# A transformer layer with experts on one core: the first chunk norms, their powers and the weight preparation reordered

## The chip, the cores and the metric

The kernel runs on one core of a Trainium2 chip. The metric is device time in microseconds (us), the median of several runs. A core has five engines that run side by side, each taking its own instructions in program order: PE (TensorE: matmuls and transposes into PSUM; PEld is its weight load), DVE (VectorE), ACT (ScalarE), POOL (GpSimd) and SP (SyncE, which here only issues DMA transfers). They wait for each other by semaphores.

## The reference

The input x is 32 sequences of 256 tokens with 128 features. It is normalised, and two branches read the result; the output is the sum of x and both. All is in float32.

```python
xn = layernorm(x)                                  # (x - m) / sqrt(v + 1e-5)
# branch A: 16 heads of 8; scores = cov(q, k)/8 + var(q) var(k)/8, softmax, Wo
# branch B:
hn   = layernorm(xn, ln1_w, ln1_b)
qkv  = hn @ in_proj_w.T + in_proj_b                # 16 heads of 8
attn = softmax(causal(q k / sqrt(8))) @ v          # over axis 0 of x: the 32 sequences are its positions
x1   = xn + attn @ out_proj_w.T + out_proj_b
hn2  = layernorm(x1, ln2_w, ln2_b)
# router: top 2 of 8 experts, gelu(hn2 @ w1[e]) @ w2[e], weighted by the gates
out  = x + A(xn) + x1 + experts(hn2)
```

The attention of branch B runs over the first axis of x, so its sequences are 32 long and there are 256 of them.

Two normalisations follow each other. With variance v of a token, the first scale is (v + eps)^-1/2. The variance of the normalised token is v/(v + eps), so the second scale is (v/(v + eps) + eps)^-1/2: both need only v.

## The kernel before, in words

The tokens are cut into 16 chunks of 512, each held as a tile of 128 partitions with four groups of 128 features (`[P, 4, P]`). `first_rounds` carries the chunks through branch B up to the router's logits in a software pipeline: its loop runs i from -2 to 15, and in one pass several chunks are at different stages. After it the heads of branch A are computed in a long loop (from about 270 us to the end), with routing, experts and combining woven in. Every engine executes its instructions in the order in which this code issues them (`manual_schedule`), so the order of the calls is the schedule.

Before the loop, in this order: `loads()` issues the DMA transfers of three chunks and the weights on the SP and ACT queues; `measure(0)` computes chunk 0's statistics; POOL casts two constants (`identb`, `causalb`); `norms(0)`; `set_in()`; `measure(1)`; `set_values(0)`.

The functions that matter:

- `measure(i)` (with `stats`): for each of the four groups a `bn_stats` and a `bn_aggr` on DVE (L262, L263; tiles sta and mva), then on POOL: add eps (L265), power -1/2 (L266), nb = -mean times scale (L274, L275), and the second scale r2 by two products, an add and a second power (L277 to L280). Eight POOL instructions of 128x4 elements each. `stats` serves the later normalisation of x1 too (stc, mvc, rsc).
- `norms(i)`: four ACT activations (L291) write the normalised tokens into zx; POOL multiplies them by r2 (L295) into zn.
- `turn_in(i)`: PE transposes the tokens (pta) and zn (ptb); ACT copies the first into xnT (L305) and scales the second into hT (L310); POOL adds the output bias `bout` to the tokens in place (L311).
- `project_in(i)`: PE computes pk, pq and pv from hT; ACT writes kb (L320), qT and v; an SP DMA writes v to DRAM, and `spread` brings it back into vb.
- `set_in()`: bk4 on DVE, four transposes of in_proj_w and out_proj_w on PE, copies to inT and outT on DVE. It then folds the value bias into the output bias: a broadcast copy bvs on DVE (L196), a product pbo on PE (L198), and an add to bout (L199).
- `set_rest()`: transposes and products of the weights of branch A on PE, with copies on DVE.
- `set_values(n)`: POOL fills v's column of ones (L244) and clears vb (L245); there are two buffers, n = 0 and 1. `set_second(n)`, in passes 3 to 5, fills the tiles of branch A on POOL (L225 to L232).
- `scores`, `lessened` (DVE: mx L374, pr L375), `exponents` (ACT), `turn_weights` (ptp, pT), `weigh` (po), `divide` (DVE: aden L412, o L413), `turn_out` (pto, oT), `project_out` (px on PE, x on DVE L426, then `stats` of x and a POOL add L429), `normalise` (POOL L436), `turn_normed`, `logits`.

A pass i issues, among other things: `load(i+5)`, `clear(i)` (an SP DMA that clears part of a DRAM buffer from the tile zero), `turn_in(i+2)`, `spread(i+1)`, `project_in(i+2)`, `project_out(i-1)`, in pass -2 `set_rest`, `set_values(1)` and the filling of zero, then `norms(i+3)`, `measure(i+4)`, `normalise(i-1)`, `scores(i+1)` and `lessened(i+1)`. So in a pass DVE has: x and the statistics of x1, then the statistics of chunk i+4, then the maxima of the next scores.

Of the kernel before, what the change touches and what calls it, by code (L numbers as in the profile page):

```python
# [11 lines left out]
F32 = mybir.dt.float32  # L12
BF16 = mybir.dt.bfloat16
I32 = mybir.dt.int32
AF = mybir.ActivationFunctionType
ALU = mybir.AluOpType
# [3 lines left out]
P = 128  # L20
NB = 32
SEQ = 256
NH, HD = 16, 8
NE, FF = 8, 256
NCHUNK = 16
# [3 lines left out]
EPS = 1e-5  # L29
# [39 lines left out]
def block_kernel(  # L69
# [21 lines left out]
    nc = tc.nc  # L91
# [6 lines left out]
    cp = ctx.enter_context(tc.tile_pool(name="cp", bufs=1))  # L98
# [26 lines left out]
    identb = cp.tile([P, P], BF16, name="identb")  # L125
    causalb = cp.tile([P, 32], BF16, name="causalb")
    bk4 = cp.tile([P, 4], F32, name="bk4")
    mhalf = cp.tile([P, 4, 1], F32, name="mhalf")
    wqkv = cp.tile([P, 3, P], F32, name="wqkv")
    wo = cp.tile([P, P], F32, name="wo")  # L130
    inT = cp.tile([P, 3, P], F32, name="inT")
# [49 lines left out]
    def set_in():  # L181
        nc.vector.tensor_scalar(bk4, cst[:, C_M4:C_M4 + 4], bk, None, ALU.mult)
        pt = bank_u([P, 4, P], "pt0")
        for n in range(3):
            nc.tensor.transpose(pt[:, n, :], ipw[:, n, :], ident)
        nc.tensor.transpose(pt[:, 3, :], opw, ident)
        nc.vector.tensor_copy(inT[:, 0:2, :], pt[:, 0:2, :])

        nc.vector.tensor_copy(
            inT[:, 2, :].rearrange("p (j g d) -> p j g d", j=4, g=4),  # L190
            pt[:, 2, :].rearrange("p (g j d) -> p j g d", j=4, g=4),
        )
        nc.vector.tensor_copy(outT, pt[:, 3, :])


        nc.vector.tensor_copy(bvs, bv.to_broadcast([P, P]))  # L196
        pbo = bank_u([P, P], "pbo")
        nc.tensor.matmul(pbo, bvs, outT, start=True, stop=True)  # L198
        nc.vector.tensor_tensor(bout, bout, pbo, ALU.add)  # L199

    def set_rest():
        pt = bank_w([P, 4, P], "pt1")
        nc.tensor.transpose(pt[:, 0, :], qkw[:, 0, :], ident)
        nc.tensor.transpose(pt[:, 1, :], qkw[:, 1, :], ident)
        nc.tensor.transpose(pt[:, 2, 0:NE], rw, ident[0:NE, 0:NE])
        nc.vector.tensor_copy(qkT, pt[:, 0:2, :])
        nc.vector.tensor_copy(rT, pt[:, 2, 0:NE])
        pb = bank_w([P, 2, P], "pqkw")
        for n in range(2):
            nc.tensor.matmul(pb[:, n, :], qkT[:, n, :], ccen, start=True, stop=True)  # L210
        nc.vector.tensor_copy(wqkv[:, 0:2, :], pb)


    NV, NQ = 3, 2
# [6 lines left out]
    def set_second(n):  # L221

        if n < NV:
            va = vaugs[n]
            nc.gpsimd.memset(va, 0.0)  # L225
            for h in range(2):
                nc.gpsimd.memset(va.rearrange("p i (m h) d -> p (i m) h d", h=2)[:, :, h, 16 + h:17 + h], 1.0)
        if n < 2:
            nc.gpsimd.memset(mts[n], 0.0)
            nc.gpsimd.memset(qkts[n], 0.0)  # L230
            for ti in range(2):
                nc.gpsimd.memset(qkts[n][:, ti, 1].rearrange("p g m r -> p (g m) r")[:, :, 9:10], 1.0)  # L232
# [7 lines left out]
    vs = [a1.tile([P, 4, 4, 4, HD + 1], F32, tag=f"v{n}", name=f"v{n}") for n in range(2)]  # L240
    vbs = [a1.tile([P, 4, 4, 16 * (HD + 1)], F32, tag=f"vb{n}", name=f"vb{n}") for n in range(2)]

    def set_values(n):
        nc.gpsimd.memset(vs[n].rearrange("p j k g d -> p (j k g) d")[:, :, HD:HD + 1], 1.0)  # L244
        nc.gpsimd.memset(vbs[n], 0.0)  # L245

    NZ = 32
# [9 lines left out]
    def stats(src, tag, i, bufs=2):  # L257

        st = a2.tile([P, 4, 6], F32, tag="st", name=f"st{tag}{i}")
        mv = a2.tile([P, 4, 2], F32, tag=f"mv{tag}", name=f"mv{tag}{i}")  # L260
        for k in range(4):
            nc.vector.bn_stats(st[:, k, :], src[:, k, :])  # L262
            nc.vector.bn_aggr(mv[:, k, :], st[:, k, :])  # L263
        rs = a2.tile([P, 4, 1], F32, tag=f"rs{tag}", name=f"rs{tag}{i}")
        nc.gpsimd.tensor_scalar(rs, mv[:, :, 1:2], EPS, None, ALU.add)  # L265
        nc.gpsimd.tensor_tensor(rs, rs, mhalf, ALU.pow)  # L266
        return mv, rs

    def measure(i):


        mv, rs = stats(xts[i], "a", i)
        nb = a2.tile([P, 4, 1], F32, tag="nb", name=f"nb{i}")
        nc.gpsimd.tensor_tensor(nb, mv[:, :, 0:1], rs, ALU.mult)  # L274
        nc.gpsimd.tensor_scalar(nb, nb, -1.0, None, ALU.mult)  # L275
        r2 = a2.tile([P, 4, 1], F32, tag="r2", name=f"r2{i}")
        nc.gpsimd.tensor_tensor(r2, rs, rs, ALU.mult)  # L277
        nc.gpsimd.tensor_tensor(r2, r2, mv[:, :, 1:2], ALU.mult)
        nc.gpsimd.tensor_scalar(r2, r2, EPS, None, ALU.add)
        nc.gpsimd.tensor_tensor(r2, r2, mhalf, ALU.pow)  # L280
        nrm[i] = rs, nb, r2

    def tokens(i):


        return zx[:, 4 * i:4 * i + 4]

    def norms(i):
        rs, nb, r2 = nrm.pop(i)
        for k in range(4):  # L290
            nc.scalar.activation(  # L291
                tokens(i)[:, k, :], xts[i][:, k, :], AF.Identity, bias=nb[:, k, :], scale=rs[:, k, :]
            )
        zns[i] = a2.tile([P, 4, P], F32, tag="zn", name=f"zn{i}")
        nc.gpsimd.tensor_tensor(zns[i], tokens(i), r2.to_broadcast([P, 4, P]), ALU.mult)  # L295

    def transposed(src, tag, i):
        pt = bank_u([P, 4, P], f"pt{tag}{i}")
        for k in range(4):
            nc.tensor.transpose(pt[:, k, :], src[:, k, :], ident)  # L300
        return pt.rearrange("p k t -> p (k t)")

    def turn_in(i):

        nc.scalar.copy(  # L305
            xnT[:, i, :].rearrange("p (c k s) -> p k c s", c=4, k=4),
            transposed(tokens(i), "a", i).rearrange("p (k c s) -> p k c s", k=4, c=4),
        )
        hTs[i] = a2.tile([P, 512], F32, tag="hT", name=f"hT{i}")
        nc.scalar.activation(hTs[i], transposed(zns.pop(i), "b", i), AF.Identity, bias=l1b, scale=l1w)  # L310
        nc.gpsimd.tensor_tensor(tokens(i), tokens(i), bout.unsqueeze(1).to_broadcast([P, 4, P]), ALU.add)  # L311

    def project_in(i):
# [137 lines left out]
    def chunk(i):  # L451
        return 0 <= i < NCHUNK

    def first_rounds():
        loads()
        nc.vector.memset(mhalf, -0.5)
        measure(0)
        nc.gpsimd.tensor_copy(identb, ident)
        nc.gpsimd.tensor_copy(causalb, cst[:, C_CAUSAL:C_CAUSAL + 32])
        norms(0)  # L460
        set_in()
        measure(1)
        set_values(0)
        for i in range(-2, NCHUNK):
            if chunk(i + 5):
                xts[i + 5] = load(i + 5)
            if 0 <= i < (NZ + 2) // 3:
                clear(i)
            if chunk(i + 2):
                turn_in(i + 2)  # L470
            if chunk(i - 1):
                weigh(i - 1, 1)
            if chunk(i):
                lessened(i, 2)
            if chunk(i - 1):
                divide(i - 1, 1)
            if chunk(i):
                lessened(i, 3)
                turn_weights(i, 0)
                turn_weights(i, 1)  # L480
                exponents(i, 1)
            if chunk(i - 1):
                turn_out(i - 1)
            if chunk(i + 1):
                spread(i + 1)
            if chunk(i + 2):
                project_in(i + 2)
            if i == NCHUNK - 1:
                project(0, 0)
                project_rest(0, 0)  # L490
            if chunk(i - 1):
                project_out(i - 1)
            if chunk(i):
                turn_weights(i, 2)
                turn_weights(i, 3)
            if i == -2:
                set_rest()
                set_values(1)
                nc.gpsimd.memset(zero, 0.0)
            if 3 <= i < 3 + NV:  # L500
                set_second(i - 3)
            if chunk(i + 3):
                norms(i + 3)
            if chunk(i + 4):
                measure(i + 4)
            if i == NCHUNK - 1:
                project(0, 1)
                project_rest(0, 1)
            if chunk(i - 1):
                normalise(i - 1)  # L510
            if chunk(i + 1):
                scores(i + 1)
            if chunk(i - 2):
                turn_normed(i - 2)
            if chunk(i + 1):
                lessened(i + 1, 0)
                lessened(i + 1, 1)
                exponents(i + 1, 0)
            if chunk(i):
                weigh(i, 0)  # L520
            if i == NCHUNK - 1:
                turn_qk(0)
            if chunk(i):
                divide(i, 0)
            if chunk(i - 2):
                logits(i - 2)
# [494 lines left out]
```

## Time and profile before

| what | value |
|---|---|
| median of three runs | 988.92 us (987.41 to 994.37) |
| the profiled execution | 992.8 us; first to last instruction (span) 991.0 us |
| mean granted TensorE clock | 0.976 of full speed |
| busy share of the span | PE 95%, DVE 71%, ACT 66%, POOL 57% |
| chain that ended last, by engine | PE 86%, DVE 7%, issue 2%, POOL 2%, ACT 1% |
| PE busy from 8 to 12, 24 to 28 and 36 to 40 us | 1.09, 1.12 and 1.52 of 4.00 us |
| POOL busy from 16 to 20, 20 to 24 and 24 to 28 us | 3.58, 4.00 and 3.75 of 4.00 us |
| POOL L295 (zn), mean of 16 | 1039 ns |
| POOL powers L266 (rsa) and L280, mean of 16 each | 1037 ns |
| ACT norms of a chunk (L291), four instructions | 1.65 us |

The busy shares are averages over stages with different limits; the change touches the first stage alone, so it is read from its rows. A line of a timeline gives the start, the duration, the engine, the line of the kernel, the operation, the tiles (written<-read), the shape and the count of merged instructions; in brackets stands how long the engine sat idle before it and what ended that. A line of the chain of waits gives start, duration and engine with tile. "issue" is time in which nothing that the profile shows was waited for.

### The profile page before, as it was taken

Reading aid. Unit: us, or ns where it says so; the run is one execution under the profiler, and the core shown is the slowest. Engines: PE = TensorE matmul, PEld = TensorE weight load, DVE = VectorE, ACT = ScalarE, POOL = GpSimd, SP = SyncE. Lnnn points to the kernel's source line nnn. Section 1 sums busy time; section 2 is a strip of 40 time slices with the busy share of each in tenths; the row PEclk is TensorE's granted clock in tenths of the full one; section 3 lists DMA queues with packets and bytes.
Section 4 is the critical chain, followed back from the end, with each engine's and each line's share of the span. In section 5 each row is a group of like instructions: output and inputs, shape, how many; then the busy total and the mean of one; then the engine's idle time right before and its main releaser. Section 6 shows DMA issues by size and latency. Waiting matters only on the chain.

```text
span 991.0 us, 32300 instructions
## 1 busy us (share of the span) xinstructions
PE 940.2 (95%) x13107; PEld 679.0 (69%) x13107; DVE 706.3 (71%) x1638; ACT 655.1 (66%) x1362; POOL 561.9 (57%) x725
## 2 busy tenths in 40 slices
PE   4788999989789999999999999999999999999998
PEld 2567777777666666666666689999866666666664
DVE  2477578667589999888888834444588888888882
ACT  4687878877446666666666665555666666676664
POOL 5468787785310002777777123333387888888870
PEclk9798999999889999999999999999999999999999
DMA  3344434422031000541111134444222321121220
GB/s 100 108 132 125 134 120 139 140 60 68 21 102 35 2 2 15 59 111 55 55 53 54 52 117 135 133 134 136 76 60 63 81 69 36 39 68 52 55 60 22
DMA packets 87747, 76.32 MB, mean 77 GB/s; under 512 B 32840, under 2 KB 70864, under 8 KB 87600
## 3 DMA queue, kind: packets, MB, share of 16 engines
q1 hardware_dynamic: 74736, 48.03, 17.4%
q0 software_dynamic: 11600, 26.10, 8.5%
q8 instruction: 103, 1.69, 0.7%
q10 hardware_dynamic: 1264, 0.14, 0.1%
q14 instruction: 44, 0.36, 0.1%
HBM read 33.98 MB, written 40.24 MB: 75 GB/s over the span
## 4 chain that ended last, share of the span: by engine, by line
PE 86%; DVE 7%; issue 2%; POOL 2%; ACT 1%; DMA 0%; ACTq 0%; DVEq 0%; SPq 0%; POOLq 0%
PE sm L610 26%; PE pav L634 13%; PE pe L854 6%; PE pp L557 6%; PE ph L845 6%; PE pqk L584 3%; PE ptp L300 2%; PE sT L616 2%; PE pt L653 2%; PE sc L359 2%; DVE pr L375 2%; PE px L834 2%; PE pk L316 2%; PE px L424 2%; PE py L687 2%
## 5 line engine op out<-in xcount | busy, mean ns | idle before, releaser
L625 ACT ACTIVATE ex<-sT 128x512 f32<-128x512 f32 x512 | 277.7, 595 | 179.0 <-PE sT L616 179.0
L622 DVE TENSOR_REDUCE mt<-sm 128x2 f32<-128x512 f32 x512 | 329.0, 686 | 73.6 <-PE sT L616 67.7
L610 PE MATMUL sm<-ka,qa 32*128 32x256 f32 x2048 | 292.4, 402 | 3.5 <-DVE mt L622 3.5
L616 PE MATMUL sT<-qa,ka 32*128 32x256 f32 x2048 | 291.0, 400 | 0.0
L610 PEld LDWEIGHTS sm<-ka,qa 32*128 32x128 f32 x2048 | 177.4, 185 | 81.0 <-issue 38.1
L616 PEld LDWEIGHTS sT<-qa,ka 32*128 32x128 f32 x2048 | 176.4, 184 | 2.6 <-issue 1.7
L801 POOL DMA_INDIRECT xsd<-zx,posi x128 | 122.9, 960 | 81.4 <-DVE posi L789 42.7
L905 POOL DMA_INDIRECT yg<-ysd,posb x128 | 122.1, 954 | 43.0 <-issue 31.5
L634 PE MATMUL pav<-ex,va 128*32 128x256 f32 x2048 | 137.2, 385 | 0.0
L859 POOL DMA_DIRECT2D ysd<-ye x71 | 48.2, 679 | 115.0 <-DVE ye L858 89.1
L634 PEld LDWEIGHTS pav<-ex,va 128*32 128x32 f32 x2048 | 53.8, 109 | 64.2 <-issue 24.0
L854 PEld LDWEIGHTS pe<-w,ge 128*128 128x128 f32 x568 | 74.5, 192 | 4.2 <-ACT ge L847 0.7
L854 PE MATMUL pe<-w,ge 128*128 128x128 f32 x568 | 74.9, 275 | 0.3 <-ACT ge L847 0.3
L845 PE MATMUL ph<-xT,w 128*128 128x256 f32 x284 | 73.3, 381 | 0.0
L557 PE MATMUL pp<-wqkv,xnT 128*128 128x384 f32 x128 | 65.6, 595 | 0.8 <-DVE mt L622 0.8
L858 DVE COPY ye<-pe 128x256 f32<-128x256 f32 x71 | 30.1, 424 | 50.8 <-PE pe L854 50.8
L837 ACT ACTIVATE xT<-px,vec 128x256 f32<-128x256 f32 x71 | 39.9, 563 | 35.8 <-PE px L834 35.8
L847 ACT ACTIVATE ge<-ph 128x512 f32<-128x512 f32 x71 | 42.4, 597 | 21.1 <-PE ph L845 21.1
L378 ACT ACTIVATE pr<-pr 128x1024 f32<-128x1024 f32 x32 | 33.8, 1058 | 34.0 <-DVE pr L375 33.9
L374 DVE TENSOR_REDUCE mx<-sc 128x16 f32<-128x512 f32 x64 | 43.4, 678 | 17.3 <-PE sc L359 17.3
L828 DVE COPY w<-wall 128x512 f32 x71 | 30.4, 429 | 33.3 <-issue 31.9
L845 PEld LDWEIGHTS ph<-xT,w 128*128 128x128 f32 x284 | 48.5, 191 | 4.1 <-ACT xT L837 0.4
(170 smaller groups left out, 1663.0 us busy)
## 6 DMA issues: line engine op xcount, KB each, us to landing
xb<-xsd SPq DMA_DIRECT2D x71, 128.0 KB, 2.1
ysd<-ye POOLq DMA_DIRECT2D x71, 128.0 KB
xsd<-zero SPq DMA_DIRECT2D x10, 852.0 KB
vald<-v SPq DMA_DIRECT2D x16, 288.0 KB, 2.3
vb<-vald SPq DMA_DIRECT2D x64, 72.0 KB, 3.0
xt<-in_L_attn_x_dram SPq DMA_DIRECT2D x64, 64.0 KB, 2.0
resd<-xt SPq DMA_DIRECT2D x64, 64.0 KB, 1.7
res<-resd SPq DMA_DIRECT2D x32, 128.0 KB, 3.3
```

What stands on the lines that cost most here:

```text
L374: nc.vector.tensor_reduce(mx, s, AX.X, ALU.max)
L557: nc.tensor.matmul(pp.rearrange("p n m -> p (n m)"), xs_all[:, ti * P:(ti + 1) * P, s], wqkv.rearrange("p n m -> p (n m)"), start=True, st ...
L610: nc.tensor.matmul(sc[:, i, :], qas[u][r:r + 32, i * P:(i + 1) * P], kas[u][r:r + 32, h, :], start=True, stop=True,)
L616: nc.tensor.matmul(sc[:, i, :], kas[u][r:r + 32, h, i * P:(i + 1) * P], qas[u][r:r + 32, :], start=True, stop=True,)
L622: nc.vector.tensor_reduce(mts[y // 8 % 2][:, :, o:o + 1], sc, AX.X, ALU.max, negate=True)
L625: nc.scalar.activation(exs[y], sc, AF.Exp, scale=1.0 / HD)
L634: nc.tensor.matmul(pos[u][32 * j:32 * j + 32, :], vaugs[s % NV][:, ti, 4 * j + 2 * g + h, :], exs[8 * u + 4 * h + j][:, ti, :], start=(h = ...
L801: yield nc.gpsimd.indirect_dma_start(xsd_views[n * NTILE + k], bass.IndirectOffsetOnAxis(ap=posi[:, k, n:n + 1], axis=0), zx[:, k, :], None,)
L845: nc.tensor.matmul(ph[:, f, :], wb[n][0][:, f * P:(f + 1) * P], xT, start=True, stop=True)
L854: nc.tensor.matmul(pe[:, j, :], ge[:, f, j * P:(j + 1) * P], w2b[:, f, :], start=(f == 0), stop=(f == 1))
L859: nc.gpsimd.dma_start(ysd[n * BLK:(n + 1) * BLK].rearrange("(p j) h -> p j h", j=2), ye)
L905: yield nc.gpsimd.indirect_dma_start(yg[s][:, ti, n, :], None, ysd, bass.IndirectOffsetOnAxis(ap=gt["posb"][:, s, ti, n:n + 1], axis=0),)
```

## The change

It does the following:

- `measure` no longer uses `stats`. DVE adds eps, negates the mean, and forms v/(v + eps) + eps (a reciprocal, a product, an add), with both sums in one tile of eight columns; POOL takes one power over the eight columns and one product for nb. mhalf grows from four columns to eight.
- `norms` of chunks 0 and 1 write the tokens by four DVE instructions in place of four ACT ones; the other chunks stay on ACT.
- The order before the loop becomes `measure(0)`, `norms(0)`, `set_in()` with `measure(1)` inside it ahead of the copy to outT, then the casts on POOL, the ones of both v buffers and the clearing of the first vb.
- The folding of the output bias becomes `set_out`, called in pass -2 behind `project_in(0)` and `norms(1)`.
- The addition of the bias to the tokens leaves `turn_in` and becomes `bias_out(i+2)`, issued behind `norms` and `measure` of the pass.
- The clearing of the second vb and the filling of zero move from pass -2 to the end of this block in pass -1.
- In pass -2 the order is norms(1), set_out, set_rest, measure(2).

```diff
-    mhalf = cp.tile([P, 4, 1], F32, name="mhalf")
+    mhalf = cp.tile([P, 8, 1], F32, name="mhalf")
...
     def set_in():
...
+        measure(1)
         nc.vector.tensor_copy(outT, pt[:, 3, :])
+
+    def set_out():
         nc.vector.tensor_copy(bvs, bv.to_broadcast([P, P]))
...
+    def set_ones(n):
+        nc.gpsimd.memset(vs[n].rearrange("p j k g d -> p (j k g) d")[:, :, HD:HD + 1], 1.0)
+
     def set_values(n):
-        nc.gpsimd.memset(vs[n].rearrange("p j k g d -> p (j k g) d")[:, :, HD:HD + 1], 1.0)
         nc.gpsimd.memset(vbs[n], 0.0)
...
     def measure(i):
-        mv, rs = stats(xts[i], "a", i)
+        st = a2.tile([P, 4, 6], F32, tag="st", name=f"sta{i}")
+        mv = a2.tile([P, 4, 2], F32, tag="mva", name=f"mva{i}")
+        for k in range(4):
+            nc.vector.bn_stats(st[:, k, :], xts[i][:, k, :])
+            nc.vector.bn_aggr(mv[:, k, :], st[:, k, :])
+        sm = a2.tile([P, 8, 1], F32, tag="sums", name=f"sums{i}")
+        nm = a2.tile([P, 4, 1], F32, tag="nm", name=f"nm{i}")
+        nc.vector.tensor_scalar(sm[:, 0:4], mv[:, :, 1:2], EPS, None, ALU.add)
+        nc.vector.tensor_scalar(nm, mv[:, :, 0:1], -1.0, None, ALU.mult)
+        nc.vector.reciprocal(sm[:, 4:8], sm[:, 0:4])
+        nc.vector.tensor_tensor(sm[:, 4:8], sm[:, 4:8], mv[:, :, 1:2], ALU.mult)
+        nc.vector.tensor_scalar(sm[:, 4:8], sm[:, 4:8], EPS, None, ALU.add)
+        rr = a2.tile([P, 8, 1], F32, tag="rr", name=f"rr{i}")
+        nc.gpsimd.tensor_tensor(rr, sm, mhalf, ALU.pow)
         nb = a2.tile([P, 4, 1], F32, tag="nb", name=f"nb{i}")
-        nc.gpsimd.tensor_tensor(nb, mv[:, :, 0:1], rs, ALU.mult)
-        nc.gpsimd.tensor_scalar(nb, nb, -1.0, None, ALU.mult)
-        r2 = a2.tile([P, 4, 1], F32, tag="r2", name=f"r2{i}")
-        nc.gpsimd.tensor_tensor(r2, rs, rs, ALU.mult)
-        nc.gpsimd.tensor_tensor(r2, r2, mv[:, :, 1:2], ALU.mult)
-        nc.gpsimd.tensor_scalar(r2, r2, EPS, None, ALU.add)
-        nc.gpsimd.tensor_tensor(r2, r2, mhalf, ALU.pow)
-        nrm[i] = rs, nb, r2
+        nc.gpsimd.tensor_tensor(nb, nm, rr[:, 0:4], ALU.mult)
+        nrm[i] = rr[:, 0:4], nb, rr[:, 4:8]
...
     def norms(i):
         rs, nb, r2 = nrm.pop(i)
         for k in range(4):
-            nc.scalar.activation(
-                tokens(i)[:, k, :], xts[i][:, k, :], AF.Identity, bias=nb[:, k, :], scale=rs[:, k, :]
-            )
+            to, x = tokens(i)[:, k, :], xts[i][:, k, :]
+            if i < 2:
+                nc.vector.tensor_scalar(to, x, rs[:, k, :], nb[:, k, :], ALU.mult, ALU.add)
+            else:
+                nc.scalar.activation(to, x, AF.Identity, bias=nb[:, k, :], scale=rs[:, k, :])
...
+    def bias_out(i):
         nc.gpsimd.tensor_tensor(tokens(i), tokens(i), bout.unsqueeze(1).to_broadcast([P, 4, P]), ALU.add)
...
         measure(0)
+        norms(0)
+        set_in()
         nc.gpsimd.tensor_copy(identb, ident)
         nc.gpsimd.tensor_copy(causalb, cst[:, C_CAUSAL:C_CAUSAL + 32])
-        norms(0)
-        set_in()
-        measure(1)
+        set_ones(0)
+        set_ones(1)
         set_values(0)
...
             if i == -2:
+                norms(1)
+                set_out()
                 set_rest()
+            if 3 <= i < 3 + NV:
+                set_second(i - 3)
+            if i == -2:
+                measure(2)
+            if 2 <= i + 3 < NCHUNK:
+                norms(i + 3)
+            if i > -2 and chunk(i + 4):
+                measure(i + 4)
+            if chunk(i + 2):
+                bias_out(i + 2)
+            if i == -1:
                 set_values(1)
                 nc.gpsimd.memset(zero, 0.0)
-            if 3 <= i < 3 + NV:
-                set_second(i - 3)
-            if chunk(i + 3):
-                norms(i + 3)
-            if chunk(i + 4):
-                measure(i + 4)
```

More of the change, by code (lines that the diff above doesn't have):

```diff
@@ L265, in stats @@
         nc.gpsimd.tensor_scalar(rs, mv[:, :, 1:2], EPS, None, ALU.add)
-        nc.gpsimd.tensor_tensor(rs, rs, mhalf, ALU.pow)
+        nc.gpsimd.tensor_tensor(rs, rs, mhalf[:, 0:4], ALU.pow)
         return mv, rs
     def measure(i):
-        mv, rs = stats(xts[i], "a", i)
-        nb = a2.tile([P, 4, 1], F32, tag="nb", name=f"nb{i}")
-        nc.gpsimd.tensor_tensor(nb, mv[:, :, 0:1], rs, ALU.mult)
-        nc.gpsimd.tensor_scalar(nb, nb, -1.0, None, ALU.mult)
-        r2 = a2.tile([P, 4, 1], F32, tag="r2", name=f"r2{i}")
-        nc.gpsimd.tensor_tensor(r2, rs, rs, ALU.mult)
-        nc.gpsimd.tensor_tensor(r2, r2, mv[:, :, 1:2], ALU.mult)
-        nc.gpsimd.tensor_scalar(r2, r2, EPS, None, ALU.add)
-        nc.gpsimd.tensor_tensor(r2, r2, mhalf, ALU.pow)
-        nrm[i] = rs, nb, r2
+        st = a2.tile([P, 4, 6], F32, tag="st", name=f"sta{i}")
[12 more added lines that the diff above has]
+        nc.gpsimd.tensor_tensor(rr, sm, mhalf, ALU.pow)
+        nb = a2.tile([P, 4, 1], F32, tag="nb", name=f"nb{i}")
+        nc.gpsimd.tensor_tensor(nb, nm, rr[:, 0:4], ALU.mult)
+        nrm[i] = rr[:, 0:4], nb, rr[:, 4:8]
     def tokens(i):
```

## The prediction, made before the changed kernel ran

> **What bounds the kernel now.** I read the page's chain of waits first (PE 86%, DVE 7%, POOL 2%), then the timeline of the first 40 us, where most of the edit lies, then the chain and the engine windows of the sixteen chunk rounds, because one edit (the statistics of a chunk) runs in every round.
>
> The beginning is a latency chain. The first score reduction on DVE starts at 35.25 us, and these lines of the timeline (start, duration, engine, line) carry what is before it:
>
> ```profile
> 11.37 1.04 POOL L295 TENSOR_TENSOR zn<-zx,r 128x512 f32<-128x512 f32 x1
> 11.46 1.02 DVE L196 COPY xnT<-vec 128x128 f32<-128x128 f32 x1
> 12.54 0.79 PE L198 MATMUL pbo<-outT,xnT 128*128 128x128 f32 x2 [1.85 <-DVE xnT L196]
> 15.91 2.07 PE L316 MATMUL pk<-hT,inT 128*128 128x512 f32 x2 [0.87 <-ACT hT L310]
> 22.52 2.05 POOL L245 MEMSET vb<- 128x2304 f32 x1
> 25.04 1.04 POOL L295 TENSOR_TENSOR zn<-zx,r 128x512 f32<-128x512 f32 x1
> 26.14 1.12 PE L300 MATMUL ptb<-cst,zn 128*128 128x128 f32 x4 [2.19 <-POOL zn L295]
> 35.25 0.69 DVE L374 TENSOR_REDUCE mx<-sc 128x16 f32<-128x512 f32 x1 [8.31 <-PE sc L359]
> ```
>
> See that PE takes the bias product (pbo) ahead of chunk 0's transposes, and that chunk 1's second transposes wait 2.19 us for POOL, which is busy with its fillings.
>
> The rounds are a closed loop through DVE. The chain of round 1 (start, us, what):
>
> ```profile
> 57.41 0.70 DVE x L426
> 58.13 0.31 DVE stc L262
> 59.82 0.31 DVE sta L262
> 61.19 0.19 DVE sta L262
> 61.58 0.59 DVE mx L374
> ...
> 66.69 0.44 DVE o L413
> 67.17 0.44 PE pto L300 x2
> 67.61 0.86 PE pk L316 x2
> 68.47 0.86 PE pq L322 x2
> 69.33 0.89 PE pv L327 x8
> 70.22 1.05 PE px L424 x8
> ```
>
> From x at 57.41 DVE works without a gap to o at 67.1; PE turns o, runs pk, pq, pv and px, and x starts again at 71.31: 13.90 us. In between lies sta, the chunk statistics. What stands just after it on DVE delays the round. The starts of x are 57.41, 71.31, 86.06, 103.46, 120.18, 135.25, 149.25, 163.38, 177.38, 193.33, 207.33, 223.31. I take 14.0 as the loop alone; the excess over it is slack for DVE: 0, 0.75, 3.4, 2.7, 1.1, 0, 0.1, 0, 1.95, 0, 2.0 us in rounds 1 to 11 (rounds 3 to 5 wait for POOL's second fillings, the others for a PE idle that the profile puts down to issue).
>
> **The change, part by part.**
>
> *One power per chunk.* POOL loses eight instructions, 3.83 us from start to start (63.49 to 67.32), and gains a power of 128x8 and a product of 0.20. The 128x4 power takes 1.04 where a 128x4 product takes 0.20: so 1.04 if that is start-up, 1.88 if it goes by element; I take 1.5. POOL saves about 2 us a round, worth nothing there: it sits idle 2.1 to 4.8 us before the L265 of each of these rounds. The chain passes POOL only by zn, which stands ahead of the removed work.
>
> DVE gains five small instructions right after sta: two scale-or-add, reciprocal, product, add. The nearest rows are 173, 172 and 155 ns for 128x8 (L757, L783, L765) and 348 ns for a 128x32 reciprocal, less for 4. From start to start a dependent pair takes 0.19 (378.38 to 378.57), an independent one 0.10 (60.22 to 60.32). 0.1+0.1+0.1+0.2+0.19+0.1 is about 0.8 us, bounds 0.5 and 1.0. All of it lies ahead of mx, where the scores are ready at about 61.1, so nothing covers it.
>
> *What they meet.* L196 above is the row that matters: a 128x128 copy within SBUF took 1.02 us where the same shape out of PSUM took 0.28 (L189), and it ended at 12.48, 0.07 us after POOL's zn (12.41). The only other such meeting is DVE's L436 at 282.14, under POOL's L429 to 282.44: its first piece lasted 378 ns against 334. The Trainium skill ("SBUF — State Buffer", section on the two separate sides) has the rule: DVE operations in a two-port mode, or with two SBUF inputs against a POOL operation that reads SBUF, share a port pair with POOL that is locked for whole instructions, and the loser fully blocks. That speaks against this change. Four of the five new instructions are of these kinds (scaling in SBUF, and a product of two SBUF operands), and in every round POOL is then busy:
>
> ```profile
> 61.24 1.28 POOL L429 TENSOR_TENSOR xt<-xt,x 128x512 f32<-128x512 f32 x1
> 61.40 0.18 DVE L263 BATCH_NORM_AGGREGATE mva<-sta 128x2 f32<-128x6 f32 x1
> 61.50 0.66 DVE L374 TENSOR_REDUCE mx<-sc 128x16 f32<-128x512 f32 x1
> 62.48 1.04 POOL L295 TENSOR_TENSOR zn<-zx,r 128x512 f32<-128x512 f32 x1
> ```
>
> The first small operation would be ready at 61.6 and wait for 62.5. If DVE keeps the port from there, mx starts at 63.25: 1.75 late. If zn takes its turn after the first, 64.3: 2.8 late. No row shows who wins; I take the middle, 2.3. Sum over rounds 1 to 11 of the delay less the slack: for 0.8 (small rows alone) 0.8+0.05+0.8+0.7+0.8+0.8 = 3.9 us; for 1.75, 10.3; for 2.3, 2.3+1.55+1.2+2.3+2.2+2.3+0.35+2.3+0.3 = 14.8; for 2.8, 19.4. Rounds 3 and 4 have fillings in the meeting too: 0.5 each, an estimate from 0.96 a filling; so 15.8. Round 0 and earlier have DVE idle there: nothing. So the row of small operations alone makes the rounds 3.9 us longer, the rule 15.8. I go with the rule, since L196 shows it here.
>
> *The beginning, chunk 0.* DVE's statistics end at 7.02, small operations to 7.85 (POOL idle, no lock), power and product to 9.7, then norms on DVE: four at 0.27 from start to start (1.15 for L436's four), so 10.9; ACT had finished at 10.80. No gain there. zn no longer stands behind two casts and six small steps: 11.0 to 12.1 instead of 12.41. PE no longer takes pbo first: ptb ends at 13.2 instead of 15.04, hT at 14.1 instead of 15.86. pk(0) starts 1.8 us earlier, and pv(0) ends at 19.2. bk4 and the inT copies follow the norms on DVE and end by 12.1, before pk needs them. ACT's table load (1.28, at 5.36) had followed a wait for the input; L625's load at 710.95 ran 2.4 us ahead of its matmul's wait, so it should run early still: 0, else +1.28.
>
> *Chunk 1.* Statistics 12.1 to 13.7, small ones 14.5, POOL power 16.1, product 16.4. norms(1) on DVE then meets casts, fillings of ones and the 2.05 vb filling: done between 18.5 and 20.6. The copy bvs follows, so pbo starts at about 20.9, and PE waits 1.7 us for it with the weights' transposes and chunk 1's queued behind. Those transposes and products took 2.1 (20.98 to 23.06); pta and ptb then run at 23.5 to between 24.4 and 25.6, hT ends 25.3 to 26.5 instead of 28.08. pk, pq and pv took 4.6 after the idle of 2.19, in windows with a granted clock of 0.60 and 0.55; in round 1 they take 2.6. Without the idle I expect the fast form, though not surely. The first mx comes 1.6 to 4.8 us earlier; I take 4.
>
> *Moved without a price, by my reading.* bias_out (1.27 each, L311) moves from ahead of L265, where POOL idles, to ahead of normalise, whose result is turned a round later; POOL's 2 us saved cover it. Filling the second vb and zero (2.05+0.57) moves to POOL after chunk 2's zn, ending near 38.5. SP's first clearing DMA waits for zero, and the spreading of chunk 1 and the next writes of v queue behind it; that lands near 44, and weigh of chunk 1 runs after 56. If that cover were gone: about 5 us once. measure(2), set_rest and loads keep their order; mhalf grows by four elements, 0.06 us.
>
> **Sum.** +15.8 in the rounds, -4 in the beginning: +11.8 on the profiled execution (992.8 us; span 991.0), 1004.6. That one stands 3.9 above the median of the runs, 988.92, so the forecast for the median is 1001. Everything after the rounds follows unchanged.
>
> **Rivals.**
> No lock for operations this small: rounds +3.9, beginning -5.5 (bvs isn't held back), so 987. For: both rows are of 128 elements. Against: nothing in L196 depends on size. This is the side that isn't slower; it decides if a small operation beside L429 lasts under 0.3 us.
> The small operations also find slack: rounds 1, beginning -7 (1.04 power, fast products): 983. Against: DVE has no gap from 57.41 to 67.1.
> POOL keeps the port through back-to-back instructions: DVE waits to the end of zn everywhere, past the fillings too: 2.8 in plain rounds, 5.2, 5.2 and 4 in rounds 3 to 5, some 25 in sum, so 1010. The records of L429 and zn overlap by 0.04, which is for it.
> The beginning gains nothing, as PE only changes its wait from zn to bvs: -1.6, so 1003; it widens the forecast.
>
> **Numbers.** Forecast with its widths (995 to 1006): 0.45; POOL keeps the port: 0.15; no lock: 0.26; small operations in slack: 0.12; other 0.02. 1% is 9.9 us, about what a measurement of this kernel tells from no change. Slower by that: two thirds of the forecast and all of the third rival, 0.44; faster 0.03; within 0.53. 984 to 1010 holds all but the ends.
>
> **What would show it.** In the changed profile: new DVE lines after sta of 0.9 us or more, ending just after L429 or zn; x to x near 16 us in rounds 1, 6, 8 and 10; first mx at 31; pbo waiting for bvs. Small operations of 0.2 us beside a busy POOL make it wrong, as would mx starting within 1 us of sta's end.

## The result and the profile after

| what | before | after |
|---|---|---|
| median | 988.91 us (987.41 to 994.37) | 1015.45 us (1015.35 to 1015.79) |
| ratio after to before, 95% interval | | 1.0255 (1.0221 to 1.0289) |
| profiled execution, span | 992.8, 991.0 us | 1015.8, 1013.8 us |
| first score maximum (mx) starts | 35.25 us | 29.23 us |
| first x starts | 57.41 us | 51.46 us |
| first x to twelfth x | 165.90 us | 193.58 us |

The changed kernel is slower by 26.5 us, above the stated range of 984 to 1010. Between the two profiled executions the difference is 23.0 us: the beginning gains 5.95, eleven rounds lose 27.68, and the rest, 1.3, falls behind them. Of the experiments below, the first four ran in a set in which every kernel, the one before too (1230.47 us), took some 240 us longer behind the rounds, so they are read by their rounds and by their difference to before.

The chain of waits of the changed kernel, by engine (before: PE 86%, DVE 7%):

```profile
PE 82%; DVE 13%; issue 1%; ACT 1%; DMA 1%; ACTq 0%; DVEq 0%; SPq 0%
```

DVE nearly doubled its share. In the changed kernel the five new DVE instructions stand on lines 284 to 288 (sums is the tile of both sums, nm the negated mean), the power and the product on POOL are L290 and L292, zn is L309, the add of x to xt is L445 and x is L442. The beginning, from the timeline of the changed kernel:

```profile
7.81 1.68 POOL L290 TENSOR_TENSOR rr<-sums,mhalf 128x8 f32<-128x8 f32 x1 [7.38 <-DVE sums L288]
9.81 1.12 DVE L305 TENSOR_SCALAR zx<-xt,rr,nb 128x128 f32<-128x128 f32 x4 [2.08 <-POOL nb L292]
11.01 1.04 POOL L309 TENSOR_TENSOR zn<-zx,rr 128x512 f32<-128x512 f32 x1 [1.23 <-DVE zx L305]
14.09 2.07 PE L332 MATMUL pk<-hT,inT 128*128 128x512 f32 x2 [0.87 <-ACT hT L324]
16.04 3.00 DVE L305 TENSOR_SCALAR zx<-xt,rr,nb 128x128 f32<-128x128 f32 x4 [1.84 <-POOL nb L292]
16.57 2.08 POOL L250 MEMSET vb<- 128x2304 f32 x1
18.97 0.21 DVE L199 COPY xnT<-vec 128x128 f32<-128x128 f32 x1
19.33 0.46 PE L201 MATMUL pbo<-outT,xnT 128*128 128x128 f32 x2
23.18 1.12 PE L332 MATMUL pk<-hT,inT 128*128 128x512 f32 x2 [0.92 <-ACT hT L324]
29.23 0.69 DVE L390 TENSOR_REDUCE mx<-sc 128x16 f32<-128x512 f32 x1 [1.49 <-PE sc L375]
```

The norms of chunk 0 take 1.12 us on DVE with POOL idle; those of chunk 1 take 3.00: POOL's filling of vb runs to 18.65, the third of the four ends at 18.79 and the last at 19.04. The copy for the bias product (L199) then takes only 0.21, so PE starts pbo at 19.33 with no wait shown. Chunk 1's pk (at 23.18) takes 1.12, where it took 2.07 before (at 28.12).

Round 8 of the changed kernel, from its timeline:

```profile
179.97 1.28 POOL L445 TENSOR_TENSOR xt<-xt,x 128x512 f32<-128x512 f32 x1
180.28 1.00 DVE L284 TENSOR_SCALAR sums<-mva 128x4 f32<-128x4 f32 x1
181.19 0.16 DVE L285 TENSOR_SCALAR nm<-mva 128x4 f32<-128x4 f32 x1
181.21 1.04 POOL L309 TENSOR_TENSOR zn<-zx,rr 128x512 f32<-128x512 f32 x1
181.31 0.18 DVE L286 RECIPROCAL sums<-sums 128x4 f32<-128x4 f32 x1
181.52 0.74 DVE L287 TENSOR_TENSOR sums<-sums,mva 128x4 f32<-128x4 f32 x1
182.30 0.17 DVE L288 TENSOR_SCALAR sums<-sums 128x4 f32<-128x4 f32 x1
182.38 0.69 DVE L390 TENSOR_REDUCE mx<-sc 128x16 f32<-128x512 f32 x1
185.82 0.18 DVE L465 COPY lg<-pl 128x32 f32<-128x32 f32 x1
186.05 1.19 PE L411 MATMUL po<-vb,pT 128*32 128x36 f32 x64 [3.01 <-DVE lg L465]
187.16 1.97 PE L314 MATMUL ptp<-cst,pr 128*128 128x128 f32 x8
```

Two things are to be seen. First, L284 lasts 1.00 us for four elements and ends at 181.28, where POOL's add ends (181.25); L287 ends at 182.26, where zn ends (182.25). mx starts 6.25 us after x (176.13), against 4.02 in this round before (x at 163.38): 2.23 later. Second, lg is late with everything else on DVE, and PE waits 3.01 us for it. Then po takes 1.19 where it took 0.76 before, and ptp 1.97 where it took 1.09. From the start of po to the next x (193.41) it is 7.36 us, against 6.33 before: 1.03 more. po starts 2.25 later in the round, and 2.25 and 1.03 make the 3.28 by which this round grew, from 14.00 to 17.28. The same places in round 8 of before:

```profile
167.40 0.66 DVE L374 TENSOR_REDUCE mx<-sc 128x16 f32<-128x512 f32 x1
171.05 0.76 PE L395 MATMUL po<-vb,pT 128*32 128x36 f32 x64
171.75 1.09 PE L300 MATMUL ptp<-cst,pr 128*128 128x128 f32 x8
```

PE's waits for lg in the changed kernel (engine, tile and line, what it waited for: us in total, times, longest); before, this line had 0.7 us in two waits:

```profile
PE po L411 <- DVE lg L465: 19.5, 9, 3.0
```

The mean of each new instruction, from the changed kernel's groups (busy us, mean ns | idle before). Alone each takes 160 to 180 ns; only the reciprocal keeps to that:

```profile
L284 DVE TENSOR_SCALAR sums<-mva 128x4 f32<-128x4 f32 x16 | 14.4, 899 | 0.8
L287 DVE TENSOR_TENSOR sums<-sums,mva 128x4 f32<-128x4 f32 x16 | 9.0, 563 | 0.6
L286 DVE RECIPROCAL sums<-sums 128x4 f32<-128x4 f32 x16 | 2.8, 178 | 0.1
```

All rounds, from x to x, with the granted clock of each stretch from the windows, and the growth that the forecast had for each:

| round | before, us | clock | after, us | clock | grew | forecast |
|---|---|---|---|---|---|---|
| 1 | 13.90 | 1.00 | 17.55 | 0.90 | 3.65 | 2.3 |
| 2 | 14.75 | 1.00 | 17.42 | 0.90 | 2.67 | 1.55 |
| 3 | 17.40 | 0.80 | 17.98 | 0.81 | 0.58 | 0.5 |
| 4 | 16.72 | 0.90 | 17.54 | 0.90 | 0.82 | 0.5 |
| 5 | 15.07 | 0.89 | 19.31 | 0.82 | 4.24 | 1.2 |
| 6 | 14.00 | 1.00 | 17.41 | 0.90 | 3.41 | 2.3 |
| 7 | 14.13 | 1.00 | 17.46 | 0.80 | 3.33 | 2.2 |
| 8 | 14.00 | 1.00 | 17.28 | 0.90 | 3.28 | 2.3 |
| 9 | 15.95 | 0.89 | 17.17 | 0.90 | 1.22 | 0.35 |
| 10 | 14.00 | 1.00 | 17.12 | 0.90 | 3.12 | 2.3 |
| 11 | 15.98 | 0.89 | 17.34 | 0.80 | 1.36 | 0.3 |
| sum | 165.90 | | 193.58 | | 27.68 | 15.8 |

Two of these stretches as the windows give them (stretch, its length, busy us and count of PE, PEld, DVE, ACT, POOL, then the clock, DMA share and GB/s), the first of before:

```profile
207.33:223.31 15.98, 14.29 (x323) 11.64 (x321) 10.68 (x30) 12.66 (x23) 11.48 (x18) 0.89 0.21 57
```

the second of the changed kernel:

```profile
176.13:193.41 17.28, 14.10 (x323) 11.60 (x321) 12.54 (x36) 11.66 (x21) 9.71 (x11) 0.90 0.37 117
```

The rounds that were long before are, but for round 2, the ones with a low clock. In the changed kernel every round has one.

### The profile page after: what moved, and what is told of

It reads as the page before. It is cut to its first block, busy times and chain, and to the rows that moved or that the text cites. A ratio compares the mean times of both kernels' runs of the same rounds, so it can differ in the third digit from the quotient of the medians.

```text
span 1013.8 us, 32291 instructions
## 1 busy us (share of the span) xinstructions
PE 947.5 (93%) x13107; PEld 685.4 (68%) x13107; DVE 737.8 (73%) x1726; ACT 652.3 (64%) x1354; POOL 538.5 (53%) x629
## 3 DMA queue, kind: packets, MB, share of 16 engines
q1 hardware_dynamic: 74736, 48.03, 16.7%
q8 instruction: 103, 1.69, 0.7%
## 4 chain that ended last, share of the span: by engine, by line
PE 82%; DVE 13%; issue 1%; ACT 1%; DMA 1%; ACTq 0%; DVEq 0%; SPq 0%
PE sm L634 26%; PE pav L658 13%; PE pe L878 6%; PE pp L581 6%; PE ph L869 6%; PE pqk L608 3%; PE ptp L314 3%; DVE pr L391 3%; PE sT L640 2%; PE pt L677 2%; DVE mx L390 2%; PE pk L332 2%; PE px L858 2%; PE py L711 1%; PE px L440 1%
## 5 line engine op out<-in xcount | busy, mean ns | idle before, releaser
L270 POOL TENSOR_SCALAR rsc<-mvc 128x4 f32<-128x4 f32 x16 | 3.8, 234 | 109.9 <-DVE mvc L268 109.9
L411 PE MATMUL po<-vb,pT 128*32 128x36 f32 x2048 | 29.8, 214 | 26.5 <-DVE lg L465 19.5
```

## The experiments

The theory after the result: the measure in the rounds costs it all; 2.2 us of each round is the meeting of the small DVE instructions with POOL's add and zn, and the rest is the pause that this makes on PE, with the lower clock behind it. Rivals: the moved POOL work (bias_out, fillings) delays something; or the five instructions cost by themselves.

**The old measure back in the rounds, the rest of the change kept.** Chunks 4 and on are measured by the eight POOL instructions again.

```diff
     def measure(i):
+        if i >= 4:
+            mv, rs = stats(xts[i], "a", i)
+            nb = a2.tile([P, 4, 1], F32, tag="nb", name=f"nb{i}")
+            nc.gpsimd.tensor_tensor(nb, mv[:, :, 0:1], rs, ALU.mult)
...
+            nrm[i] = rs, nb, r2
+            return
```

> The changed kernel, but chunks 4 to 15 (those measured inside the rounds) get their scales on POOL by the old eight instructions; chunks 0 to 3 keep the new ones, and every other part of the change stays. Theory (the five new DVE instructions wait for POOL's port in each round, and the PE pause that follows halves its clock for a time): the rounds go back to the 14 to 17 us of before and the 6.0 us won in the beginning stay: 983 us, within 980 to 986. Rival (the moved bias addition, the later filling or the order of the passes makes the rounds longer): 1005 us or more.

Measured: 1225.18 us, ratio 0.9953 (0.9938 to 0.9968), 5.3 us less than before. First x at 52.63, first to twelfth x 167.5 us. The rounds are those of before; the beginning keeps its gain.

**The new measure alone, in the kernel before.**

```diff
-        mv, rs = stats(xts[i], "a", i)
...
+        nc.vector.tensor_scalar(sm[:, 0:4], mv[:, :, 1:2], EPS, None, ALU.add)
...
+        nc.gpsimd.tensor_tensor(rr, sm, mhalf, ALU.pow)
```

> The kernel before with the new measure alone (five DVE instructions, one power over eight columns), nothing moved. Theory: the rounds cost what they cost in the changed kernel, +27.7 us from the first x to the twelfth, and the beginning changes by less than 2 us: 1016 us, within 1012 to 1020. Rival (the cost needs the moved parts): under 1000 us.

Measured: 1259.22 us, ratio 1.0243 (1.0219 to 1.0267), 28.8 us more. First x at 57.49, as before; first to twelfth x 191.8 us. One part of the change makes the whole loss, and the moved POOL work is not needed for it.

**POOL's add to xt moved away.** The add and its DMAs are issued behind bias_out.

```diff
+
+    def add_in(i):
         xt = xts.pop(i)
-        nc.gpsimd.tensor_tensor(xt, xt, x1, ALU.add)
+        nc.gpsimd.tensor_tensor(xt, xt, x1s[i], ALU.add)
...
                 bias_out(i + 2)
+            if chunk(i - 1):
+                add_in(i - 1)
```

> The changed kernel with one POOL instruction moved: the addition of x1 to the residual, with the DMAs that send it, goes behind the bias addition of the pass, so that POOL has less in hand when DVE reaches the five new instructions. All instructions are kept. Theory (POOL's port, not the number of instructions, makes the delay): the first of the five falls from 0.9 to 0.17 us, mx starts 0.8 us after the statistics rather than 2.2, rounds near 15 us, 988 us, within 984 to 994. Rival (five more instructions on DVE cost this by themselves): 1013 us or more. If the two-operand product still meets zn, some 0.9 us a round remain: about 997.

Measured: 1243.7 us, ratio 1.0106 (1.0082 to 1.0131), first to twelfth x 184.4 us. That is 13.2 us above before, where at most 8 were expected: from round 3 on the meeting didn't go, as zn moved up into the place of the add. From its timeline, round 7:

```profile
156.45 1.04 POOL L309 TENSOR_TENSOR zn<-zx,rr 128x512 f32<-128x512 f32 x1
156.66 0.85 DVE L284 TENSOR_SCALAR sums<-mva 128x4 f32<-128x4 f32 x1
157.76 0.16 DVE L287 TENSOR_TENSOR sums<-sums,mva 128x4 f32<-128x4 f32 x1
```

L284 is held until zn ends (157.49), and the product, with POOL idle, takes 0.16. In rounds 6, 8 and 10 it is the other way round: L284 takes 0.17 and the product 0.80 to 0.89, to the end of zn. In rounds 1 and 2 neither is held; they last 14.81 and, with a break of 2.44 us on PE within po, 16.73. One meeting less is worth 9 us over the rounds (193.6 to 184.4). The low clock stayed: 0.80 to 0.90 in every round, 0.90 and 0.81 in the two from 169.98 to 204.32, which lasted 16.57 and 17.77.

**PE kept busy in its pause.** From chunk 3 on the four transposes of zn are made five times, with the same result; everything else is the changed kernel.

```diff
-        for k in range(4):
-            nc.tensor.transpose(pt[:, k, :], src[:, k, :], ident)
+        for _ in range(5 if tag == "b" and i >= 3 else 1):
+            for k in range(4):
+                nc.tensor.transpose(pt[:, k, :], src[:, k, :], ident)
```

> The changed kernel with PE given more to do: from chunk 3 on the four transposes of zn are made five times over, into the same place, in the stretch in which PE waits for a PSUM bank. Theory (the pause of 3 us halves PE's clock, so that the eight transposes ptp after it take 1.97 us for 1.0): the granted clock of the rounds rises from about 0.9 to 1.0, ptp falls to about 1.1, and eleven rounds lose about 1.0 us each: 1005 us, within 1001 to 1009. Rival (ptp is long for another reason, or the clock doesn't matter there): 1015 us or more.

Measured: 1249.39 us, ratio 1.0156 (1.0122 to 1.0190). It was run again where before took 991.95:

> The kernel of e4 once more, for the same reason. Its rounds came down to 16.2 us where the clock stayed at 1.00. Theory (the port alone makes the delay of 2.2 us a round, the clock some 1.0 more): 17 to 20 us above before, where the changed kernel is 25 above.

Measured: 1011.09 us, ratio 1.0188 (1.0142 to 1.0234). Sixteen more transposes a round make the kernel no slower than the change but faster: ratios of 1.0156 and 1.0188 against 1.0255, 19 us above before in both sets instead of 26.5, though the second interval overlaps that of the change. First to twelfth x is 187.1 and 187.8 us, for 193.6. Clearer is the single round. The windows of round 10, then its timeline in that round, both of the second run:

```profile
208.01:224.25 16.24, 14.93 (x338) 11.92 (x337) 12.54 (x35) 11.68 (x22) 9.71 (x11) 1.00 0.20 56
```

```profile
215.13 2.35 PE L315 MATMUL ptb<-cst,zn 128*128 128x128 f32 x20
217.92 0.76 PE L412 MATMUL po<-vb,pT 128*32 128x36 f32 x64 [0.45 <-DVE lg L466]
218.61 1.09 PE L315 MATMUL ptp<-cst,pr 128*128 128x128 f32 x8
```

DVE is held as in the changed kernel (L284 takes 1.00, L287 0.74), but PE's pause is 0.45 us, the clock is 1.00, and po and ptp have their old durations. po starts 9.91 us after x, as in the changed kernel (9.92), and from there to the next x it is 6.33 us, as before. The round lasts 16.24: the 14.00 of before and 2.24, which is the delay of mx. So the 1.03 us are PE's pause by way of the clock. Rounds 1, 3, 4 and 6 to 8 of this run still had 0.82 to 0.91 and lasted 16.7 to 19.4. In round 6 PE paused 1.02 us within po, before the repeated transposes; these then ran slowly (3.45 us); in rounds 7 and 8 they did so too (3.64 and 3.83) without such a pause.

**The five instructions without the meeting.** They are issued behind the first two maxima and differences (mx, pr), and bias_out and normalise behind the power, so that POOL is idle while they run.

```diff
-            if i > -2 and chunk(i + 4):
-                measure(i + 4)
...
+            if i >= 0 and chunk(i + 4):
+                measure_first(i + 4)
...
                 exponents(i + 1, 0)
+            if i >= 0 and chunk(i + 4):
+                measure_last(i + 4)
+                bias_out(i + 2)
+                if chunk(i - 1):
+                    normalise(i - 1)
```

> The changed kernel with the five new DVE instructions kept in every round but placed behind the two maxima and differences of the next scores, where POOL has finished zn; POOL's bias addition and normalise of the pass are issued behind the new power, so that POOL is idle when the five run. The number of instructions is the same. Theory (the meeting with POOL costs, and the clock follows from the pause): all five take 0.15 to 0.2 us, a round is 14.8 to 15.2 us, and with the 5 to 6 us of the beginning the time is that of before, within 6 us either way. Rival (five more DVE instructions in the loop, wherever they stand, cost 2 us or more a round): 20 us or more above before.

Measured: 992.99 us against 990.18, ratio 1.0031 (1.0014 to 1.0048); first to twelfth x 169.8 us. From its timeline:

```profile
152.04 0.16 DVE L290 TENSOR_SCALAR sums<-mva 128x4 f32<-128x4 f32 x1
152.44 0.16 DVE L293 TENSOR_TENSOR sums<-sums,mva 128x4 f32<-128x4 f32 x1
152.64 0.17 DVE L294 TENSOR_SCALAR sums<-sums 128x4 f32<-128x4 f32 x1
152.89 1.65 POOL L296 TENSOR_TENSOR rr<-sums,mhalf 128x8 f32<-128x8 f32 x1 [1.45 <-DVE sums L294]
154.37 1.09 PE L324 MATMUL ptp<-cst,pr 128*128 128x128 f32 x8
```

The five cost 0.68 us together (152.04 to the next instruction at 152.72), and this round lasts 14.69. Only in rounds 3 to 5, behind the fillings, are some of the five still held (0.51 to 0.96 us). A plain round is thus 14.00 before, 14.69 with the five alone, 16.24 with the meeting too, and 17.1 to 17.6 with the low clock.

**The measure ahead of x.** DVE idles 2.94 us before x in a plain round of before, while PE runs pk to px. So the statistics of chunk i+4 were placed there, once with the old eight POOL instructions, once with the five on DVE:

```diff
+            if i >= 0 and chunk(i + 4):
+                measure(i + 4)
             if chunk(i - 1):
                 project_out(i - 1)
...
-            if i > -2 and chunk(i + 4):
-                measure(i + 4)
+            if i == -1:
+                measure(3)
```

> The kernel of e1 (old eight POOL instructions for chunks 4 to 15) with the whole statistics of chunk i+4 placed ahead of project_out on DVE, where DVE waits 2.9 us for px. Theory (the rounds are a loop through DVE, in which the statistics stand): the loop loses 1.7 us, rounds fall to about 13, and the time is 10 to 18 us under before. Rival (PE or POOL holds the rounds at 14 us once DVE is out of the way): 4 to 6 us under before, as e1.

Measured: 980.31 us, ratio 0.9908 (0.9883 to 0.9932), first to twelfth x 157.0 us, plain rounds of 13.1 to 13.9. It beats both kernels, at 9.9 us under before; but the loop lost some 0.5 us a round, not the 1.7 of the theory, and what holds it there stays open.

> The changed kernel (five DVE instructions, one power) with the whole measure of chunk i+4 placed ahead of project_out on DVE. There POOL runs normalise, so the five should each wait for a piece of it (0.8 us). Theory: statistics and five instructions take 4 to 5 us where DVE had 2.9 to 4 us to spare, the loop keeps about its old length, and the time is from 10 us under before to 5 above. If the five don't wait there, it equals e5.

Measured: 983.46 us, ratio 0.9931 (0.9910 to 0.9951), first to twelfth x 163.4 us. The meeting with normalise, which was expected, doesn't come in any round. From its timeline:

```profile
141.03 0.17 DVE L284 TENSOR_SCALAR sums<-mva 128x4 f32<-128x4 f32 x1
141.45 0.16 DVE L287 TENSOR_TENSOR sums<-sums,mva 128x4 f32<-128x4 f32 x1
141.96 1.67 POOL L290 TENSOR_TENSOR rr<-sums,mhalf 128x8 f32<-128x8 f32 x1 [2.60 <-DVE sums L288]
```

POOL had been idle for 2.60 us when its power began, and all five took 0.16 to 0.18 us each. With the change's measure unaltered, its place alone decides between 983 and 1015.

**The fillings of branch A behind normalise**, in the kernel with the measure ahead of x (POOL's version).

```diff
-            if 3 <= i < 3 + NV:
-                set_second(i - 3)
...
                 normalise(i - 1)
+            if 3 <= i < 3 + NV:
+                set_second(i - 3)
```

> The kernel of e5 with the second fillings of rounds 3 to 5 issued on POOL behind normalise, no more ahead of zn. In e5 these rounds take 17.7, 15.1 and 13.9 us, for 13.5 of the plain ones. Theory (they wait for zn, which stands behind the fillings): about 13.5 to 14.5 each, 4 to 5 us less than e5, so 13 to 15 us under before. Rival (these rounds are long for the PE pause and clock alone): as e5.

Measured: 982.31 us against 991.95, ratio 0.9910 (0.9878 to 0.9941): no gain over 0.9908, where 4 to 5 us were expected. Rounds 3 and 4 fell from 17.7 and 15.1 us to 13.6 and 13.5, at a clock of 1.00, but round 5 rose from 13.9 to 15.9 (0.89) and round 11 from 13.6 to 15.7; first to twelfth x is 155.7. In rounds 5 and 11 PE breaks off within po, for 1.61 and 1.35 us. The long rounds moved rather than went.

**Norms of chunks 0 and 1 on ACT again**, in the kernel with the old measure in the rounds (`if i < 2` becomes `if i < 0`), and that kernel itself once more, for the size of the beginning's gain.

> The kernel of e1 with the norms of chunks 0 and 1 left on ACT. It tells what the move of these norms is worth in the beginning: chunk 0's four take 1.65 on ACT for 1.12 on DVE; chunk 1's have to wait on ACT behind kb, qT and v of chunk 0 to about 20 us, but are spared the wait for POOL's fillings. Expected: 1 to 3 us above e1, still 2 to 4 under before.

> The kernel of e1 once more, since in its first set every kernel, the one before too, took some 240 us longer in a stage after the rounds. Theory: 4 to 6 us under before, the gain of the beginning with the rounds as they were.

Measured: 986.10 us, ratio 0.9960 (0.9943 to 0.9977), first x at 53.85, with ACT; 986.56 us, ratio 0.9943 (0.9929 to 0.9957), first x at 52.23, with DVE. The place of the norms is worth 1.2 to 1.6 us at the first x, which the medians don't tell apart; the beginning as a whole is worth 5 to 6.

## Why the prediction was wrong

**The meeting and its size: right.** The forecast had the first small instruction wait for the end of the add, and took 2.3 us of delay between two bounds; mx is 2.23 us later. By the records DVE gets its turn when the add ends and runs two instructions; then zn has its turn, and the product waits for zn. What kept this from the upper bound is that nm and the reciprocal are done before zn ends. The five alone were put at 0.8 and are 0.68 us. The rule of the Trainium skill ("SBUF — State Buffer", two separate sides) was the better guide than the rows of small operations, which gave 3.9 us for all rounds.

**The step that failed: the "Sum over rounds 1 to 11 of the delay less the slack", which charged a round with DVE's delay alone, 2.3 us.** The sum came to 15.8 us and measured 27.68. It carried the delay of DVE along unchanged; it didn't ask what a late DVE does to PE's speed. The plain rounds lost 3.1 to 3.7 us, 3.28 in round 8.

- In rounds 1, 6, 7, 8 and 10, where the slack was put at 0 or 0.1, the forecast had 11.4 us and 16.79 were lost. The difference, about 1.1 a round, is by round 8 what the pause on PE (3.01 us there) does to the clock behind it: keeping PE busy brought round 10 to 16.24.
- In rounds 2 to 5, 9 and 11 the forecast had 4.4 us and 10.89 were lost, again 1.1 a round. The slack itself was there. In round 9 PE breaks off within its first po (46 products, then 18) in both kernels, and what it loses in that break it needn't wait for afterwards. The break before, then the break and the wait for lg in the changed kernel:

```profile
183.80 0.36 PE L395 MATMUL po<-vb,pT 128*32 128x36 f32 x18 [1.65 <-issue]
```

```profile
199.44 0.38 PE L411 MATMUL po<-vb,pT 128*32 128x36 f32 x18 [1.44 <-issue]
203.32 1.19 PE L411 MATMUL po<-vb,pT 128*32 128x36 f32 x64 [1.58 <-DVE lg L465]
```

  1.44 and 1.58 make the 3.0 of the plain rounds, and the round lasts 17.17 like them. With 3.28 us in place of 2.3 and the slack taken off as in the forecast, rounds 2, 9 and 11 come to 2.53, 1.33 and 1.28; they grew by 2.67, 1.22 and 1.36.

By the same working all eleven rounds come to 25.2 us, so this one number is 9.4 of the 11.9 that were missing. Of the other 2.5, 2.1 are in round 5. The forecast gave rounds 3 and 4 half a microsecond for their fillings and round 5 none; there mx is 3.32 us late, for 2.52 in rounds 3 and 4. The rest of round 5 stays open. The slack is not the same in each execution, though: the kernel with the old measure, run twice, took 15.63 and 14.01 us for round 9, with a break of 1.26 and 0.80 in po, and 14.00 and 16.10 for round 11, with one of 0.90 and 1.80.

With 2.0 more gained in the beginning and 1.3 behind the rounds, the 11.9 account for the 11.2 us between the forecast for the profiled execution, 1004.6, and 1015.8.

**The beginning: right in sign, small in size.** It gave 5.95 us, where 4 were taken, between bounds of 1.6 and 4.8. pk(0) at 14.09 and the power of eight columns (1.64 to 1.68, between the bounds) came as forecast, and chunk 0's norms on DVE gained nothing by themselves. The norms of chunk 1 were held by the vb filling, as forecast, and ended at 19.04, inside 18.5 to 20.6. But "PE waits 1.7 us for bvs" was wrong: the norms ended near the early end, the copy took 0.21, and PE was busy with pv until 19.27. The fast form of chunk 1's products came.

**Moved at no price: held.** With the old measure back, the moved bias_out, filling and zero left the rounds at 163.2 and 167.5 us against 165.9. ACT's table load ran at 4.76, before its data, and cost nothing.

**The rivals.** No lock, and small operations in slack: refuted by L284's mean of 899 ns. "POOL keeps the port through back-to-back instructions" gave 1010, nearest to the time, by the wrong way: in plain rounds DVE had its turn between the add and zn. Only in the filling rounds was it part of the truth, as the last section shows.

## What to carry to other kernels

An instruction's price on a busy engine depends on what the other engine of its port is doing then: move it to where that engine is idle before asking how long it takes (983 against 1015 us here, with the same instructions). When rounds of one loop differ in length, look at the granted clock of each and at where PE breaks off. A pause that a late engine makes on PE costs its own length and then the slower products behind it, so ask of each delay which engine it starves and for how long.

## What the hardware showed that was not expected

- Four elements a partition are held for as long as POOL's whole instruction runs, or two of them. In a filling round of the changed kernel, by its timeline:

```profile
90.26 1.28 POOL L445 TENSOR_TENSOR xt<-xt,x 128x512 f32<-128x512 f32 x1
90.57 1.89 DVE L284 TENSOR_SCALAR sums<-mva 128x4 f32<-128x4 f32 x1
91.48 0.95 POOL L228 MEMSET va<- 128x1024 f32 x1
91.48 0.98 DVE L285 TENSOR_SCALAR nm<-mva 128x4 f32<-128x4 f32 x1
92.49 0.18 DVE L286 RECIPROCAL sums<-sums 128x4 f32<-128x4 f32 x1
92.57 0.31 POOL L232 MEMSET mt<- 128x256 f32 x1
92.70 0.16 DVE L287 TENSOR_TENSOR sums<-sums,mva 128x4 f32<-128x4 f32 x1
```

  L284 takes 1.89 us: it is held through the add and the filling of va. Here POOL by the records kept its turn from one instruction to the next, while in round 8 L284 came in between the add and zn; but nm starts at 91.48 all the same, about where the add ends (91.54), so L284 may have been served in part by then. The filling held L284 and nm, which have one SBUF input; the product of two ran in 0.16 while mt was filled, and was held by zn and by bias_out, which read SBUF (0.74 in round 8, 1.12 in the beginning beside L327). What decides the turn stays open.
- The pause that lowers the clock can be short: the slow po and ptp followed a wait of 3.01 us in the changed kernel, and one of 1.69 in round 11 of before. The Trainium skill ("TensorE: Matmul & The Clock Gate", Part 1) has the clock fall after an idle window of about 3.4 us; both pauses are shorter, and here the measurement decides. Which pause suffices isn't settled, and the length of one pause doesn't tell it. With the five instructions ahead of x, a slow po (1.19) followed a break of 0.79 us within po in round 11; with the fillings behind normalise, none followed a break of 1.75 in round 7. The kernel with repeated transposes still had rounds at 0.82 to 0.91.
